# A macaron block with a selective scan: even feed-forward tiles beside the scan steps, and finer, pinned side work

## The chip, the cores and the metric

The kernel runs on one core of one Trainium2 chip. The metric is device time in microseconds (us), the median of three runs. TensorE (PE in the profile, its weight loads PEld) multiplies; VectorE (DVE), ScalarE (ACT) and GpSimd (POOL) do the rest; SyncE (SP) issues all of the loop's DMAs from one queue, in order. The engines run side by side, and each takes its own instructions in order.

## The reference

For x of 4 sequences of 1024 rows and 512 columns, all in float32:

```python
x = x + 0.5 * ffn(layernorm(x))
x = x + mamba(layernorm(x))
x = x + 0.5 * ffn(layernorm(x))          # the same weights as the first

# ffn, inner width 1408
hdn = silu((xf @ gate_w.T) * gate_s) * ((xf @ up_w.T) * up_s)
out = (hdn @ down_w.T) * down_s

# mamba, inner width 1024, state 16
h, gate = split(x @ W_in.T)
h = silu(causal_conv_4_taps(h) + conv_b)
ts, Bm, Cm = split(h @ Wx.T)              # widths 128, 16, 16, each RMS-normed
delta = softplus(ts @ Wdt.T + dt_bias)
s = exp(delta * A) * s + delta * Bm * h   # over the time steps, s is 1024 x 16
y = (s . Cm + D * h) * silu(gate)
out = y @ Wout.T
```

## The kernel before, in words

**Steps.** The 4096 rows are 16 scan steps (`k`, NCS) of 256 rows (T), four to a sequence; a row tile has 128 rows, two to a step. A step has 8 channel tiles of 128 channels (`i`, NI), and each of these 4 units (`g`, NS), so 32 units a step. A unit (`unit`, L517) covers 128 channels and four of the 16 states: states and channels are laid over the partitions, with `rep` holding delta and delta*h of a channel tile four times and `bc` holding B and C. Per unit ACT makes `da` = exp(A*delta) in PSUM (L533, 4 instructions of 256 columns), POOL makes `sb` = delta*h*B (L536, 2 of 512), DVE scans (L540, 4), ACT keeps the last column as `state` (L545), DVE multiplies by C into `pr` (L546, 2), and one unit later PE sums the states with the `fold` matrix into `yps` (`add_up`, L556). After the fourth unit DVE adds D*h into `u` (L562). `gated` (L566, POOL) multiplies `u` by the gate `g`. There are four `da` and four `sb` buffers (two units), three `pr`.

**Work beside the scan.** Everything else is a list of `Work` parts, each with a cost for PE and for DVE. `background(k)` writes the list of step k, and the loop at L738 takes parts from it after each unit as long as the PE cost done lies behind the DVE cost done, or as the next step's parameters must be ready (by unit 22 of 32). The list of step k holds:
- the gate projection of this step (`gate`, L505, ACT copies L509 and one Silu L511), and the output projection of the step before (`tail`, L585, rows written to DRAM as `x2`);
- for step k+1: layer norm, transposes, input projection with the convolution (`prep_conv`, L354, L358, L365), and the small projection with its norms (`prep_params`, L389 to L434), whose last part `turn` stores B and C to DRAM and loads them back, spread over the partitions, as `bc`;
- a feed-forward pass `FFN`: gate products (L243, ACT L257, Silu L262), up products (L243, DVE L274), down products (L291), then `tmp` (L301, DVE) and the sum on POOL (L305). A pass takes up to 512 rows, and its weights (22 + 11 blocks of 256 KB) are loaded anew for each pass.

**Which rows the passes take.** A pass is made of halves of 256 rows, of the first feed-forward (stage 1, which must come before a row's scan) or the second (stage 2, after it). The front has one half; step 0 has two of stage 1; step 1 has one; steps 2 to 13 have one of each stage; step 14 has two of stage 2; step 15 has one; after the last step one is left. In numbers of 128-row tiles: 2, then 4, 2, 4 (x13), 2, then 2. Steps 14 and 15 (`late`) use an order of their own, with the output projection first.

**Softplus.** `head(k, i)`, issued after unit 1 of each odd channel tile for the two tiles three ahead, emits two `dp` products (L461), ACT's Abs, Relu, Exp and Ln (L466 to L469). `rest`, issued one unit later, emits five POOL operations in a row (L472 to L476). `rows` stores the result to DRAM one channel tile later, after unit 1, and `spread` loads it as `rep` at the end of that tile.

**Order.** A scheduler sets the final order of each engine's instructions from priorities, except for those given to `pin`, which keep the order in which they were written. `defer(n, f)` calls f after n more parts that have a PE cost; `settle` calls all that wait. Layer norm (`stats`): DVE statistics (L186, L187), three tiny POOL operations (L188 to L190), and a deferred, pinned ACT instruction (L192); `flip` then transposes on PE (L204), and ACT copies out of PSUM (L207).

Of the kernel before, what the change touches and what calls it, by code (L numbers as in the profile page):

```python
# [13 lines left out]
P = 128  # L14
# [12 lines left out]
Q = 32  # L27
# [5 lines left out]
LEAD = 13  # L33
RING = 15
# [3 lines left out]
def macaron_kernel(ctx: ExitStack, tc: tile.TileContext, a: dict, out: bass.AP):  # L38
# [140 lines left out]
    def stats(src, name):  # L179
# [8 lines left out]
        nc.gpsimd.tensor_scalar(ve, mv[:, 1:2], EPS, None, ALU.add)  # L188
        nc.gpsimd.tensor_tensor(rs, ve, neg_half[:, 0:1], ALU.pow)
        nc.gpsimd.tensor_scalar(nb, mv[:, 0:1], rs, -1.0, ALU.mult, ALU.mult)  # L190
        xn = p3.tile([P, H], F32, tag="xn", name=f"xn{name}")
        cell = [xn, lambda: pin(nc.scalar.activation(xn, src, AF.Identity, bias=nb, scale=rs))]  # L192
        defer(1, lambda: cell[1] and (cell[1](), cell.__setitem__(1, None)))
        return cell

    def flip(cell, dst, name, more=lambda: None):

        xn, norm = cell
        if norm:
            norm()  # L200
            cell[1] = None
# [10 lines left out]
    class FFN:  # L212


        def __init__(self, name, halves):
            self.name, self.halves = name, halves
            self.n = len(halves) * T
            self.x = {}

        def load(self, h):  # L220
            if self.halves[h][0] == 2:
                settle()
                write()
            stage, c = self.halves[h]
            for j in range(J):
                r = c * J + j
                t = self.x[h, j] = p8.tile([P, H], F32, tag="xf", name=f"xf{self.name}_{h}_{j}")
                load(out=t, in_=a["x"][r * P : (r + 1) * P, :] if stage == 1 else x2[r])

        def stats(self, h, j):  # L230
            return stats(self.x[h, j], f"f{self.name}_{h}_{j}")

        def flip(self, xn, h, j):
            if not hasattr(self, "xT"):
                self.xT = p1.tile([P, KH, 2 * T], F32, tag="fxT", name=f"fxT{self.name}")
            o = h * T + j * P
            flip(xn, self.xT[:, :, o : o + P], f"f{self.name}_{h}_{j}")
# [42 lines left out]
        def down(self):  # L280
            parts = [(h, j) for h in range(len(self.halves)) for j in range(J)]
            wd = []

            def part(h, j):
                def emit(w=None):
                    wd.extend(w or [])
                    nm = f"{self.name}_{h}_{j}"
                    op = ps_m.tile([P, H], F32, tag="mm", name=f"fo{nm}")
                    o = h * T + j * P
                    for it in range(NF):  # L290
                        nc.tensor.matmul(  # L291
                            op, lhsT=self.hd[:, it, o : o + P], rhs=wd[it],
                            start=(it == 0), stop=(it == NF - 1),
                        )
                    x = self.x[h, j]
                    tmp = p2.tile([P, H], F32, tag="tmp", name=f"tmp{nm}")
                    stage, c = self.halves[h]
                    r = c * J + j
# [11 lines left out]
                return Work(NF * H, H, emit, [("down_w", it) for it in range(NF)] if h + j == 0 else ())  # L310

            r = [part(h, j) for h, j in parts]
# [65 lines left out]
    def prep_params(k):  # L378
# [46 lines left out]
        def turn():  # L425
# [11 lines left out]
            load(out=row.rearrange("g s t -> (g s) t"), in_=bcT)  # L437
            bc = d["bc"] = p2.tile([P, BC // S, T], F32, tag="bc", name=f"bc{k}")
            for s in range(S):
                load(  # L440
                    out=bc[s * Q : (s + 1) * Q],
                    in_=row[:, s, :].unsqueeze(0).to_broadcast([Q, BC // S, T]),
                )
            d["ready"] = True
# [3 lines left out]
    def head(k, i):  # L448

# [10 lines left out]
        for q in range(2):  # L460
            nc.tensor.matmul(  # L461
                dp[:, q, :], lhsT=w_dt[:, (i + q) * P : (i + q + 1) * P], rhs=d["tsT"],
                start=True, stop=True,
            )
        for q in range(2):
            nc.scalar.activation(z[:, q, :], dp[:, q, :], AF.Abs, bias=dt_b[:, i + q : i + q + 1])  # L466
            nc.scalar.activation(dd[:, q, 0, :], dp[:, q, :], AF.Relu, bias=dt_b[:, i + q : i + q + 1])  # L467
# [14 lines left out]
    def rest(k, i):  # L482

        st[k]["rest", i]()
# [160 lines left out]
    def late(k):  # L645

        return k >= NCS - 2
# [208 lines left out]
```

## Time and profile before

| | us |
|---|---|
| median of 3 runs (3403.05 to 3404.28) | 3403.47 |
| the profiled execution, its own time | 3408.67 |
| its span, first to last instruction | 3406.6 |
| PE / DVE / ACT / POOL busy | 3156.1 / 2434.9 / 2001.4 / 2034.4 |
| DMA traffic | 504.59 MB, mean 148 GB/s |

The profile is of one execution. Busy time is the union of an engine's instructions. In a group's row, the number after the bar is busy time, then the mean ns of one instruction, then the idle time of the engine just before it and what ended it. A line of the waits reads: who waited, for whom, us in total, times, the longest. In the row of a stretch of time, each engine's busy time stands with its number of instructions, then the mean granted TensorE clock as a share of full speed, then the DMA share. In a row in order of time, the bracket at the end is the idle time before it and who ended that. One matrix product in float32 shows as two equal pieces in the profile.

### The profile page before, as it was taken

The numbers are of one execution on the slowest core, as the hardware profiler recorded it, in microseconds if no ns is written. First come the engines' busy times: TensorE is split into PE (matmuls) and PEld (weight loads), VectorE is DVE, ScalarE is ACT, GpSimd is POOL, SyncE is SP. The second block draws the span as 40 slices with busy tenths as digits, with TensorE's granted clock in tenths as the row PEclk, the third lists the DMA queues.
The fourth block names the chain that finished last, engine by engine and source line by source line (L and its number), as shares of the span: only waits on it lengthen the run. The fifth ranks groups of instructions, "written<-read, shape, count | busy, mean of one in ns | idle before, by whom it ended". The sixth has DMA issues, their size and how long they took to land. (4 is left out here: it accounts for less than half of the span.)

```text
span 3406.6 us, 41741 instructions
## 1 busy us (share of the span) xinstructions
PE 3156.1 (93%) x12448; PEld 1609.4 (47%) x12448; DVE 2434.9 (71%) x4202; ACT 2001.4 (59%) x4395; POOL 2034.4 (60%) x1959
## 2 busy tenths in 40 slices
PE   8897676999999999999999999999999999989898
PEld 5534352544444454444445454444545444344445
DVE  1177686687868778786877778687786779757781
ACT  2446654756656575766657475765747576465551
POOL 1266655566665756666575666757566576655760
PEclk9997787999999999999999999999999999999899
DMA  6345454546555554656565465556546555643643
GB/s 201 97 125 138 136 137 123 147 129 185 146 163 156 155 156 117 189 138 171 142 171 161 118 180 137 161 142 171 163 124 177 130 161 142 186 114 100 192 136 105
DMA packets 286417, 504.59 MB, mean 148 GB/s; under 512 B 31984, under 2 KB 50160, under 8 KB 286192
## 3 DMA queue, kind: packets, MB, share of 16 engines
q1 hardware_dynamic: 284608, 501.47, 53.3%
q8 instruction: 100, 1.64, 0.2%
q14 instruction: 125, 1.02, 0.1%
q10 hardware_dynamic: 1584, 0.45, 0.1%
HBM read 442.56 MB, written 59.24 MB: 147 GB/s over the span
## 5 line engine op out<-in xcount | busy, mean ns | idle before, releaser
L536 POOL TENSOR_TENSOR sb<-rep,bc 128x512 f32<-128x512 f32 x1024 | 1280.4, 1273 | 466.0 <-DVE da L540 441.5
L540 DVE TENSOR_TENSOR_SCAN da<-da,state,sb 128x256 f32<-128x256 f32 x1536 | 1060.1, 739 | 263.5 <-ACT da L533 203.4
L533 ACT ACTIVATE da<-rep,a_w 128x256 f32<-128x256 f32 x2048 | 901.3, 470 | 266.2 <-DVE pr L546 249.4
L546 DVE TENSOR_TENSOR pr<-da,bc 128x512 f32<-128x512 f32 x1024 | 667.4, 677 | 77.8 <-ACT state L545 61.8
L243 PE MATMUL up_w<-fxT,w_up_w 128*128 128x512 f32 (+1 forms) x1408 | 607.0, 578 | 18.7 <-issue 13.7
L243 PE MATMUL gate_w<-fxT,w_gate_w 128*128 128x512 f32 (+1 forms) x1408 | 608.5, 577 | 9.6 <-ACT hd L257 4.8
L291 PE MATMUL fo<-w_down_w,hd 128*128 128x512 f32 x1320 | 587.4, 597 | 0.0
L556 PE MATMUL yps<-pr,fold 128*32 128x256 f32 x4096 | 386.6, 401 | 140.0 <-DVE pr L546 117.7
L545 ACT COPY state<-da 128x2 f32<-128x2 f32 x768 | 118.9, 161 | 498.6 <-DVE da L540 490.5
L243 PEld LDWEIGHTS up_w<-fxT,w_up_w 128*128 128x128 f32 x1408 | 260.5, 192 | 304.4 <-issue 288.3
L243 PEld LDWEIGHTS gate_w<-fxT,w_gate_w 128*128 128x128 f32 x1408 | 265.5, 193 | 283.8 <-issue 250.7
L540 DVE TENSOR_TENSOR_SCAN da<-da,sb 128x256 f32<-128x256 f32 x512 | 321.1, 679 | 96.5 <-ACT da L533 69.8
L291 PEld LDWEIGHTS fo<-w_down_w,hd 128*128 128x128 f32 x1320 | 244.6, 191 | 291.3 <-issue 282.7
L556 PEld LDWEIGHTS yps<-pr,fold 128*32 128x32 f32 x4096 | 105.0, 109 | 481.8 <-DVE pr L546 225.7
L472 POOL TENSOR_SCALAR e<-z 128x512 f32<-128x512 f32 x64 | 124.4, 1944 | 214.0 <-ACT z L468 204.9
L505 PE MATMUL gp<-mxT,w_W_in 128*128 128x256 f32 x1024 | 248.7, 392 | 1.9 <-ACT dd L467 1.1
L354 PE MATMUL hp<-mxT,w_W_in 128*128 128x259 f32 x1024 | 244.2, 388 | 5.7 <-issue 2.0
L585 PE MATMUL op<-w_Wout,u 128*128 128x512 f32 x512 | 234.6, 606 | 8.1 <-POOL sb L536 5.3
L365 DVE SCALAR_TENSOR_TENSOR u<-hp,conv_w,u 128x256 f32<-128x256 f32 x384 | 175.1, 473 | 71.2 <-ACT u L358 67.7
L354 PEld LDWEIGHTS hp<-mxT,w_W_in 128*128 128x128 f32 x1024 | 190.0, 190 | 62.3 <-issue 25.3
L505 PEld LDWEIGHTS gp<-mxT,w_W_in 128*128 128x128 f32 x1024 | 190.7, 192 | 57.2 <-issue 21.8
L566 POOL TENSOR_TENSOR u<-u,g 128x256 f32<-128x256 f32 x128 | 92.8, 730 | 196.4 <-DVE u L562 196.2
(114 smaller groups left out, 2744.5 us busy)
## 6 DMA issues: line engine op xcount, KB each, us to landing
rep<-row SPq DMA_DIRECT2D x512, 256.0 KB, 5.6
w_W_in<-in_W_in_dram SPq DMA_DIRECT2D x256, 256.0 KB, 3.1
w_gate_w<-in_gate_w_dram SPq DMA_DIRECT2D x198, 256.0 KB, 3.4
w_up_w<-in_up_w_dram SPq DMA_DIRECT2D x198, 256.0 KB, 3.0
w_down_w<-in_down_w_dram SPq DMA_DIRECT2D x198, 256.0 KB, 2.9
row<-dd SPq DMA_DIRECT2D x128, 256.0 KB, 4.5
w_Wout<-in_Wout_dram SPq DMA_DIRECT2D x128, 256.0 KB, 4.3
bc<-bcd SPq DMA_DIRECT2D x64, 256.0 KB, 4.7
```

Source lines behind the costliest of these rows:

```text
L243: nc.tensor.matmul(o[:, : self.n], lhsT=w[:, k, :], rhs=self.xT[:, k, : self.n], start=(k == 0), stop=(k == KH - 1),)
L291: nc.tensor.matmul(op, lhsT=self.hd[:, it, o : o + P], rhs=wd[it], start=(it == 0), stop=(it == NF - 1),)
L354: nc.tensor.matmul(hp[:, : K - 1 + T], lhsT=w[:, kk, :], rhs=st[k]["xnT"][:, kk, :], start=(kk == 0), stop=(kk == KH - 1),)
L365: pin(nc.vector.scalar_tensor_tensor(u[:, i, :], hp[:, q : q + T], conv_w[:, i, q : q + 1], u[:, i, :], ALU.mult, ALU.add,))
L472: pin(nc.gpsimd.tensor_scalar(e, z, 1.0, 1.0, ALU.add, ALU.subtract))
L505: nc.tensor.matmul(gp[:, :T], lhsT=w[:, kk, :], rhs=st[k]["xnT"][:, kk, K - 1 :], start=(kk == 0), stop=(kk == KH - 1),)
L533: nc.scalar.activation(da[:, j, :], rep[:, h + j, 0, :], AF.Exp, scale=a_w[:, b0 + h + j, g : g + 1])
L536: nc.gpsimd.tensor_tensor(sb, rep[:, hs, 1, :], d["bc"][:, g : g + 1, :].to_broadcast([P, 2, T]), ALU.mult)
L540: nc.vector.tensor_tensor_scan(da[:, j, :], da[:, j, :], sb[:, j, :], 0.0 if first else state[:, b0 + h + j, g : g + 1], ALU.mult, ALU.add,)
L546: nc.vector.tensor_tensor(pr[:, hs, :], da, d["bc"][:, NS + g : NS + g + 1, :].to_broadcast([P, 2, T]), ALU.mult)
L556: nc.tensor.matmul(yp[j * Q : (j + 1) * Q, :], lhsT=fold, rhs=pr[:, j, :], start=(g == 0), stop=(g == NS - 1),)
L585: nc.tensor.matmul(op, lhsT=st[k]["u"][:, i, j * P : (j + 1) * P], rhs=wo[i], start=(i == 0), stop=(i == NI - 1),)
```

## The change

Five things change.

1. The feed-forward passes are made of single 128-row tiles in order of rows. Steps 1, 3, 5, 8, 10 and 12 (`THREE`) get three tiles, all others four, and the pass after the last step four: in tiles 2 (front), then 4, 3, 4, 3, 4, 3, 4, 4, 3, 4, 3, 4, 3, 4, 4, 4, then 4. Steps 14 and 15 lose their own order. The last two rows of the output projection stay in SBUF for the last pass instead of going through DRAM. The gate projection of step 0 moves from the front to the list of step 0.
2. `head` returns a list of eight parts (two of them empty), called `chores`. The first is called after unit 1, the others one by one in the middle of each half unit, before `pr`. Its ACT instructions are pinned. `rows` follows one unit later than before (after unit 2).
3. `stats` emits its POOL operations one part later and its ACT instruction two parts later, all pinned.
4. `gated` is pinned, and the last four channel tiles are always gated in the first units of the next step.
5. The store and the four loads of B and C are deferred by two and three parts.

```diff
-        nc.gpsimd.tensor_scalar(ve, mv[:, 1:2], EPS, None, ALU.add)
-        nc.gpsimd.tensor_tensor(rs, ve, neg_half[:, 0:1], ALU.pow)
-        nc.gpsimd.tensor_scalar(nb, mv[:, 0:1], rs, -1.0, ALU.mult, ALU.mult)
         xn = p3.tile([P, H], F32, tag="xn", name=f"xn{name}")
-        cell = [xn, lambda: pin(nc.scalar.activation(xn, src, AF.Identity, bias=nb, scale=rs))]
-        defer(1, lambda: cell[1] and (cell[1](), cell.__setitem__(1, None)))
+        def roots():
+            pin(nc.gpsimd.tensor_scalar(ve, mv[:, 1:2], EPS, None, ALU.add))
+            pin(nc.gpsimd.tensor_tensor(rs, ve, neg_half[:, 0:1], ALU.pow))
+            pin(nc.gpsimd.tensor_scalar(nb, mv[:, 0:1], rs, -1.0, ALU.mult, ALU.mult))
+        left = [roots, lambda: pin(nc.scalar.activation(xn, src, AF.Identity, bias=nb, scale=rs))]
+        def more():
+            if left:
+                left.pop(0)()
+                defer(1, more)
+        defer(1, more)
...
-            load(out=row.rearrange("g s t -> (g s) t"), in_=bcT)
+            def out_of():
+                load(out=row.rearrange("g s t -> (g s) t"), in_=bcT)
+            def back_in():
+                for s in range(S):
+                    load(out=bc[s * Q : (s + 1) * Q], in_=...)
+            defer(2, out_of)
+            defer(3, back_in)
...
     def head(k, i):
+        return [
+            products,
+            split,
+            logs,
+            lambda: None,
+            lambda: None,
+            lambda: pin(nc.gpsimd.tensor_scalar(e, z, 1.0, 1.0, ALU.add, ALU.subtract)),
+            correct,
+            complete,
+        ]
...
     def unit(k, i, g):
+            if chores:
+                chores.pop(0)()
             nc.vector.tensor_tensor(pr[:, hs, :], da, ...)
...
     def gated(k, i):
-        nc.gpsimd.tensor_tensor(u, u, g_all[:, i, :], ALU.mult)
+        pin(nc.gpsimd.tensor_tensor(u, u, g_all[:, i, :], ALU.mult))
...
-    beside = {0: [(1, 1), (1, 2)]}
-    for k in range(1, NCS):
-        beside[k] = ([(1, k + 2)] if k + 2 < NCS else []) + ([(2, k - 2)] if k >= 2 else [])
-    beside[NCS - 2].append((2, NCS - 3))
-    beside[NCS - 1] = [(2, NCS - 2)]
+    first = [(1, r) for r in range(J, NCS * J)]
+    second = [(2, r) for r in range((NCS - 1) * J)]
+    for k in range(NCS):
+        m = 3 if k in THREE else 4
+        ones = min(len(first), 4 if k == 0 else 3 if k == 1 else 2)
+        twos = m - ones
+        beside[k] = [first.pop(0) for _ in range(ones)] + [second.pop(0) for _ in range(twos)]
+    last = second + [(2, r) for r in range((NCS - 1) * J, NCS * J)]
...
-    front += [turn_m[0], gate_0[2]] + turn_m[1:] + weave(prep_conv(0), gate(0))[0]
+    front += [turn_m[0], gate_0[2]] + turn_m[1:] + prep_conv(0)
...
-                if i == 0 and k and not late(k):
+                if i == 0 and k:
                     gated(k - 1, NI - NS + g)
...
-                if i % 2 == 0 and g == 1 and k2 < NCS:
+                if i % 2 == 0 and g == 2 and k2 < NCS:
                     rows(k2, i2)
                     rows(k2, i2 + 1)
...
-                if i % 2 == 1 and g == 2 and k2 < NCS:
-                    rest(k2, i2)
                 if i % 2 == 1 and g == 1 and k2 < NCS:
-                    head(k2, i2)
+                    chores += head(k2, i2)
+                    chores.pop(0)()
```

The parts of `head` hold the same instructions as before: `products` the two `dp` products, `split` Abs and Relu, `logs` Exp and Ln, `correct` and `complete` two POOL operations each.

## The prediction

> **What bounds the kernel now.** I read the page first, then the busy times by stage, then the waits of one stage, then its instructions in order of time. The page:
>
> ```profile
> span 3406.6 us, 41741 instructions
> PE 3156.1 (93%) x12448; PEld 1609.4 (47%) x12448; DVE 2434.9 (71%) x4202; ACT 2001.4 (59%) x4395; POOL 2034.4 (60%) x1959
> PE   8897676999999999999999999999999999989898
> PEclk9997787999999999999999999999999999999899
> ```
>
> TensorE is busy 93% on average, but slices 4 to 7 (about 255 to 595 us) have 6 or 7 tenths and a clock of 7 or 8 tenths. So there are two kinds of steps. I cut the span at the last `u` (L562) of each step; rows are for step 1, steps 3 and 4, 14, 15, and what follows step 15:
>
> ```profile
> core 0: us, PE busy (x) PEld busy (x) DVE busy (x) ACT busy (x) POOL busy (x), PEclk, DMA share, GB/s
> 376.00:573.20 197.20, 137.36 (x604) 74.12 (x604) 149.86 (x259) 108.11 (x265) 118.61 (x116) 0.81 0.53 153
> 780.90:976.10 195.20, 190.49 (x755) 93.85 (x754) 152.74 (x263) 119.34 (x228) 127.42 (x123) 1.00 0.57 154
> 976.10:1172.80 196.70, 190.47 (x757) 94.09 (x756) 146.37 (x262) 125.37 (x288) 126.50 (x123) 1.00 0.57 155
> 2947.70:3164.10 216.40, 198.26 (x746) 95.88 (x745) 149.36 (x255) 124.95 (x282) 122.79 (x115) 0.96 0.49 136
> 3164.10:3327.40 163.30, 140.93 (x612) 75.76 (x611) 131.27 (x215) 90.53 (x175) 103.09 (x89) 0.91 0.56 158
> 3327.40:3406.60 79.20, 64.46 (x236) 45.52 (x236) 10.87 (x21) 12.04 (x19) 7.81 (x11) 0.92 0.33 103
> ```
>
> Steps 3 to 13 (195 to 199 us each) are TensorE's: idle under 6 us, full clock. Step 1 has half of their feed-forward columns, 53 us less of PE, and takes as long: 60 us of PE idle and a clock of 0.81. Steps 14 and 15 lie between. Where step 1 loses its time:
>
> ```profile
> PE yps L556 <- DVE pr L546: 54.2, 20, 6.5
> POOL u L566 <- DVE u L562: 25.3, 7, 6.1
> ACT z L466 <- PE dp L461: 24.2, 2, 16.5
> DVE da L540 <- ACT da L533: 14.0, 4, 10.9
> DVE da L540 <- POOL sb L536: 13.0, 9, 2.9
> ```
>
> PE waits for the scan (DVE), the scan for `sb` from POOL and `da` from ACT, and these stand behind something else. In order of time, in step 1:
>
> ```profile
> 516.07 1.66 PE L556 MATMUL yps<-pr,fold 128*32 128x256 f32 x8 [6.32 <-DVE pr L546]
> 518.34 0.73 POOL L566 TENSOR_TENSOR u<-u,g 128x256 f32<-128x256 f32 x1 [4.98 <-DVE u L562]
> 520.32 0.76 DVE L540 TENSOR_TENSOR_SCAN da<-da,state,sb 128x256 f32<-128x256 f32 x1 [2.06 <-POOL sb L536]
> 524.22 1.06 PE L556 MATMUL yps<-pr,fold 128*32 128x256 f32 x2 [6.49 <-DVE pr L546]
> ```
>
> The gating `u` on POOL waits 5 us for a `u` just being made, the `sb` behind it come late, the scan starts late, PE stands 6.5 us. The 6.32 us before it follow a softplus burst on POOL (L472 to L476, 503.7 to 512.1 us). PE's gaps of 3.5 to 6.7 us in this step are of these two kinds, or follow ACT's 16.5 us behind `dp`.
>
> **The size of one feed-forward tile.** The end of the chain:
>
> ```profile
> 3363.63 18.99 PE up_we L243 x88
> ```
>
> 88 pieces of 256 columns in 18.99 us: 0.216 us each; the 44 pieces `foe` of 512 columns take 19.0 us (0.432). Time goes by columns, so dividing the same 64 tiles differently removes no PE time; the passes stay 18, so weights are as many. One tile of 128 rows costs 176 gate/up pieces x 0.108 = 19.0, 22 down pieces x 0.432 = 9.5, transposes 0.4: 28.9 us of PE, 2.8 us of DVE (an eleventh share of `hd`, 0.69 `tmp`, 0.83 statistics), some 2 us each of ACT and POOL.
>
> **The change part by part** (us, against the profiled span of 3406.6).
>
> Even tiles. Steps 3, 5, 8, 10, 12 go from four tiles to three; step 1 from two to three; step 15 from two to four; the end from two to four; others keep four. A three-tile step needs 190.5 - 28.9 = 161.6 of PE and about 152 - 3 = 149 of DVE. I counted both kernels' instruction orders between the eight `yps` sums of a step and priced them with the rows: three-tile step, PE 18, 17, 32, 22, 18, 27, 13, 15; DVE (raised 7% to meet its measured busy time) 13, 14, 28, 20, 18, 29, 7, 16. The larger of each pair sums to 165. The same count gives 192 for a four-tile step that measures 196 to 197 (+5), but 150 for step 1, which measures 197 (+47), and 141 for step 15, which measures 163 (+22). So the question is the overhead on 165. I take +11, 176, nearer the four-tile rows, because PE still leads in most tiles and both kinds of stalls are edited (next). Five steps take 984.9 now: 880, -105. Step 1, same load: 177, -20.
>
> Here a rule speaks against the change. Trace: step 1, with its PE gaps of 3.5 to 6.7 us, ran at a clock of 0.81, which is 75 of its 197 us at half rate, and the steps without such gaps at 1.00; at 0.81 a three-tile step would need 161.6/0.81 = 199.5, and nothing would be won. The Trainium skill, "TensorE: Matmul & The Clock Gate", section "Why this matters for your kernels", says gaps above about 3 us drop the clock to half. Taking matmuls out of a step uncovers such gaps. By rule and row of step 1 the five steps bring nothing; at the 0.96 of step 14 they need 168. I stay near the second, since the long gaps have named causes that go.
>
> Softplus in eight parts. No instruction more: per head 2 `dp` pairs, 4 + 2 ACT, 5 POOL (1.94 + 4 x 1.27 = 7.0). `e` now stands 2.5 units after `dp` and, in three of four heads of the new order, an `sb` stands between its POOL parts; at tile 0 nine POOL operations (11 us) still stand together. POOL's wait for `z` (204.9 us in all) goes mostly; ACT's wait for `dp` gets half a unit of distance. Pinned ACT work may make PE's FFN wait for the PSUM bank of `dp`: 0 to 2 a step, in the +11. `row` stores are issued one unit later (5.5 us); they land in 4.5, `rep` in 5.6, and the `rep` is wanted four units (22 us) after its issue: 0, and if that cover were gone POOL and ACT would start the tile late. Seven more table loads, 7 x 1.28 = 9 us on ACT, which is 60% busy: 0.
>
> Gating pinned. In the old order 110 of 128 gatings wait for a fresh DVE result, in the new one 10. POOL's 196.2 us behind `u` go; in PE-bound steps that buys nothing. What is late next is `xf` behind `tmp` (187.8 us on POOL), which the change leaves.
>
> Norms in three. Same instructions, POOL's three and the norm one part later each. POOL's 54.5 us behind `mvf` shrink; a flip may find its norm late: PE waits 12.8 us for that in all now, bound -5 to +5, take 0.
>
> B and C later. Five DMAs move two or three parts (about 4 us each) back on SP. SP's 224.9 us behind `bcT` go; PE waits for no weight transfer anywhere, so 0. They are wanted at the next step, some six units (33 us) on.
>
> Front and step 0. Eight `gp` products (64 pieces x 0.216 = 13.8 of PE) and the gate's Silu go from the front into step 0: -12 there, as PE leads that stretch; step 0 has 41 us of PE idle and fewer stalls, 196 to 188: -8. Step 2 began cold after step 1 (207.7): -11. Step 14 loses its special order and becomes a four-tile step (216.4 to 196): -20. Step 15: count 163 for PE, plus 9: 172, +9.
>
> End. Now 15.4 us from the last `u` to `gate_we`, 57 of matmuls, 5 after. The `x2` store and reload goes (5.3 us of it waiting for the load): about 10, plus 176 x 0.429 + 88 x 0.432 = 113.5, plus 5: 128.5, +49 (say +50).
>
> Sum: -105 -20 -12 -8 -11 -20 +9 +50 = -117, span 3289.6. The profiled run took 3408.67, 2.1 more than its span and 5.2 more than the median 3403.47; on the median's footing 3286.5.
>
> **The rivals.**
> Half the stalls stay: three-tile steps at 187, the overhead of step 15 on 165. Tile 0's burst and `xf` speak for it. Five steps -50, step 1 -10: in all -52, 3351.
> The stalls go entirely: 168, as tight as four tiles. The free end of step 15, where a unit takes 3.8 us of pure DVE, speaks for it. The five -145, step 1 -29, step 0 -14, rest -12 -11 -20 +5 +49: -177, 3226.
> The other side: a step with fewer matmuls isn't shorter, as step 1 shows. The in-order queues lock PE to the scan, PE's gaps pass 3.4 us, half clock holds 196 to 197. Then the six steps bring 0, step 15 takes 196 (+33), the end +50, against -51 elsewhere: +32, 3435. It decides from about 195.5 us per three-tile step, where the six no longer pay the net +8 of the rest.
> That the scheduler undoes the edit is excluded by the order counted above, but for tile 0.
>
> **How the numbers follow.** Likeliest case 0.50 (3286, own range 3260 to 3320), half the stalls 0.22, none 0.15, the other side 0.11, near cancellation 0.02. 0.2% is 6.8 us, about what a measurement of this kernel can tell from no change. Faster 0.86, same 0.03, slower 0.11. The range 3225 to 3372 leaves out the slower side and part of the two middle rivals' far halves.
>
> **What would show it.** Right: three-tile steps of 170 to 182 us with clock above 0.95 and PE idle about 12; POOL's waits of `u` and `e` near zero; step 14 near 196; an end near 128. Wrong: three-tile steps with a clock near 0.8 or PE waiting 40 us for `pr`; four-tile steps over 200; long waits of `da` for `rep` or `bc`.

## The result, and the profile after

The changed kernel takes 3435.47 us (median of 4 runs, 3433.95 to 3437.15) beside 3403.55 for the kernel before: 1.0094 times as long, 95% interval 1.0076 to 1.0111. The forecast was 3286.0, between 3225 and 3372, and faster. The page:

```profile
span 3432.2 us, 41676 instructions
PE 3190.5 (93%) x12448; PEld 1612.8 (47%) x12448; DVE 2434.3 (71%) x4202; ACT 2008.9 (59%) x4402; POOL 2028.4 (59%) x1959
PE   8897699999989998999999899999999899999999
PEclk9998799999999999999999999999999999999999
```

In TensorE's row slices 4 and 5 (about 257 to 429 us) still have 7 and 6 tenths, but the rest of step 1 is filled; yet the span grew by 25.6 us. By steps, cut again at the last `u` (now L588): steps 1, 3, 4, 5, 6, 14, 15, and the end.

```profile
core 0: us, PE busy (x) PEld busy (x) DVE busy (x) ACT busy (x) POOL busy (x), PEclk, DMA share, GB/s
368.90:562.70 193.80, 163.03 (x666) 81.86 (x666) 150.43 (x260) 116.93 (x278) 129.21 (x124) 0.91 0.58 161
770.00:958.00 188.00, 172.14 (x734) 92.09 (x732) 145.62 (x253) 120.77 (x228) 123.67 (x119) 0.95 0.60 164
958.00:1163.80 205.80, 193.96 (x754) 95.32 (x755) 151.05 (x268) 122.84 (x290) 127.25 (x122) 0.98 0.52 142
1163.80:1348.30 184.50, 173.52 (x734) 91.45 (x732) 145.54 (x253) 124.31 (x283) 120.66 (x116) 0.98 0.61 169
1348.30:1558.20 209.90, 198.07 (x757) 96.64 (x758) 159.19 (x271) 126.48 (x294) 132.57 (x129) 0.97 0.51 139
2923.40:3123.90 200.50, 193.10 (x757) 94.84 (x756) 153.91 (x263) 127.28 (x287) 126.88 (x122) 0.99 0.54 151
3123.90:3291.30 167.40, 166.40 (x625) 73.12 (x624) 131.94 (x212) 92.45 (x171) 100.64 (x83) 1.00 0.52 145
3291.30:3432.20 140.90, 132.60 (x312) 58.81 (x312) 15.23 (x23) 19.30 (x23) 12.41 (x19) 0.98 0.21 66
```

Steps 3 and 5 have three tiles and are shorter (188.0 and 184.5); steps 4 and 6 have the tiles they had before and went from 196.7 and 196.9 to 205.8 and 209.9. All steps, in us:

| part | before | predicted change | after | change |
|---|---|---|---|---|
| front and step 0 | 376.0 | -20 | 368.9 | -7 |
| step 1 | 197.2 | -20 | 193.8 | -3 |
| step 2 | 207.7 | -11 | 207.3 | 0 |
| three-tile steps 3, 5, 8, 10, 12 | 984.9 | -105 | 917.7 | -67 |
| four-tile steps 4, 6, 7, 9, 11, 13 | 1182.0 | 0 | 1235.7 | +54 |
| step 14 | 216.4 | -20 | 200.5 | -16 |
| step 15 | 163.3 | +9 | 167.4 | +4 |
| end | 79.2 | +50 | 140.9 | +62 |
| sum | 3406.6 | -117 | 3432.2 | +26 |

Two rows hold most of the error: the four-tile steps (54) and the three-tile steps (38); then step 1 (17), the front (13), the end (12) and step 2 (11). What TensorE waits for in step 4, before and after:

```profile
PE yps L556 <- DVE u L562: 1.5, 1, 1.5
```

```profile
PE yps L582 <- DVE u L588: 3.4, 1, 3.4
PE gate_w L252 <- ACT fxT L217: 3.6, 1, 3.6
```

And VectorE in order of time just ahead of such a `u` in step 6: of the kernel before the scans alone, of the kernel after all up to the `u`:

```profile
1551.40 2.03 DVE L540 TENSOR_TENSOR_SCAN da<-da,state,sb 128x256 f32<-128x256 f32 x3
```

```profile
1540.08 3.32 DVE L564 TENSOR_TENSOR_SCAN da<-da,state,sb 128x256 f32<-128x256 f32 x5
1543.30 0.68 DVE L307 TENSOR_TENSOR tmp<-fo,ds 128x512 f32<-128x512 f32 x1
1543.89 0.47 DVE L588 SCALAR_TENSOR_TENSOR u<-u,d_w,yps 128x256 f32<-128x256 f32 x1
```

The next channel tile's `yps` goes into the one PSUM tile that `u` reads, so TensorE stands until five scans (three before), a `tmp` and the `u` are through. (The tile has two halves, used in turn by the channel tiles, so by the profile the wait is for the tile and not for the same data; two separate tiles were not tried.) GpSimd's waits over the whole run, one of before and three of after, and its longest on a transfer in step 1:

```profile
POOL sb L536 <- DVE da L540: 441.5, 261, 15.7
```

```profile
POOL sb L560 <- DVE da L564: 574.1, 320, 14.4
POOL e L505 <- ACT z L486: 172.1, 37, 10.7
POOL u L592 <- DVE u L588: 16.1, 2, 11.1
```

```profile
379.02 1.26 POOL L560 TENSOR_TENSOR sb<-rep,bc 128x512 f32<-128x512 f32 x1 [20.04 <-DMA bc<-bcd]
```

The gating's wait fell from 196.2 us to 16.1, as predicted; the softplus's only from 204.9 to 172.1; and `sb`'s wait for the scan rose from 441.5 to 574.1: what GpSimd no longer waits for elsewhere it waits for the scan. The last row is new: B and C of step 1, written later, are 20 us late. GpSimd's waits for `rep` grew too, from 6.4 us to 31.5 (five times, the longest 7.7), where the prediction saw full cover; but step lengths don't follow them (with softplus parts and pin alone, see below, step 7 has such a wait of 6.0 us and takes 198.1 us, step 8 has none and takes 198.0).

### The profile page after: what moved, and what is told of

It is laid out like the page before. It is cut to its first block, busy times and chain, and to the rows that moved or that the text cites. A ratio compares the mean times of both kernels' runs of the same rounds, so it can differ in the third digit from the quotient of the medians.

```text
span 3432.2 us, 41676 instructions
## 1 busy us (share of the span) xinstructions
PE 3190.5 (93%) x12448; PEld 1612.8 (47%) x12448; DVE 2434.3 (71%) x4202; ACT 2008.9 (59%) x4402; POOL 2028.4 (59%) x1959
## 5 line engine op out<-in xcount | busy, mean ns | idle before, releaser
L560 POOL TENSOR_TENSOR sb<-rep,bc 128x512 f32<-128x512 f32 x1024 | 1286.4, 1272 | 699.5 <-DVE da L564 574.1
L252 PE MATMUL up_w<-fxT,w_up_w 128*128 128x512 f32 (+1 forms) x1408 | 585.8, 561 | 14.3 <-issue 9.4
L298 PE MATMUL fo<-w_down_w,hd 128*128 128x512 f32 x1276 | 579.7, 608 | 0.0
L582 PE MATMUL yps<-pr,fold 128*32 128x256 f32 x4096 | 396.1, 399 | 150.1 <-DVE pr L572 105.3
L582 PEld LDWEIGHTS yps<-pr,fold 128*32 128x32 f32 x4096 | 105.3, 109 | 486.1 <-DVE pr L572 207.0
L505 POOL TENSOR_SCALAR e<-z 128x512 f32<-128x512 f32 x64 | 124.3, 1942 | 190.0 <-ACT z L486 172.1
L360 PEld LDWEIGHTS hp<-mxT,w_W_in 128*128 128x128 f32 x1024 | 191.4, 191 | 57.9 <-issue 20.4
L311 POOL TENSOR_TENSOR xf<-xf,tmp 128x512 f32<-128x512 f32 x58 | 73.3, 1269 | 163.7 <-DVE tmp L307 163.7
```

Source lines behind the costliest of these rows:

```text
L252: nc.tensor.matmul(o[:, : self.n], lhsT=w[:, k, :], rhs=self.xT[:, k, : self.n], start=(k == 0), stop=(k == KH - 1),)
L298: nc.tensor.matmul(op, lhsT=self.hd[:, it, t * P : (t + 1) * P], rhs=wd[it], start=(it == 0), stop=(it == NF - 1),)
L360: nc.tensor.matmul(hp[:, : K - 1 + T], lhsT=w[:, kk, :], rhs=st[k]["xnT"][:, kk, :], start=(kk == 0), stop=(kk == KH - 1),)
L505: lambda: pin(nc.gpsimd.tensor_scalar(e, z, 1.0, 1.0, ALU.add, ALU.subtract)),
L560: nc.gpsimd.tensor_tensor(sb, rep[:, hs, 1, :], d["bc"][:, g : g + 1, :].to_broadcast([P, 2, T]), ALU.mult)
L582: nc.tensor.matmul(yp[j * Q : (j + 1) * Q, :], lhsT=fold, rhs=pr[:, j, :], start=(g == 0), stop=(g == NS - 1),)
```

## The experiments

Step lengths in all of them are cut at the last `u`. "Full steps" are steps 3 to 13 with four tiles each. Ratios are to the kernel before on the same chip, with the 95% interval.

### Which half of the change costs: the tiles alone, the small edits alone

Theory A: the tiles lose, because a three-tile step gives its saving back at the boundary. Theory B: the tiles pay and the finely issued side work costs. The kernel with the even tiles alone (the changed kernel with the other edits undone):

```diff
-            if chores:
-                chores.pop(0)()
...
-        pin(nc.gpsimd.tensor_tensor(u, u, g_all[:, i, :], ALU.mult))
+        nc.gpsimd.tensor_tensor(u, u, g_all[:, i, :], ALU.mult)
...
-            defer(2, out_of)
-            defer(3, back_in)
+            out_of()
+            back_in()
```

> The kernel before with the even tiles alone (and what belongs to them: no special order in steps 14 and 15, the step-0 gate products moved, the last rows kept in SBUF); softplus, norms, gating and B/C as before. Theory A (the tiles lose: what a three-tile step saves, the four-tile step after it gives back at the step boundary, and the end grows): 3435 to 3460 us, four-tile steps after three-tile ones still near 205 to 210. Theory B (the finer, pinned side work lengthens the TensorE-bound steps by 3 to 10 us each and the tiles alone would pay): 3370 to 3400, four-tile steps back at 196.

Measured 3533.11 us, ratio 1.038 (1.0364 to 1.0395). Steps 5, 6 and 8 (three, four and three tiles):

```profile
1181.00:1380.40 199.40, 172.90 (x731) 91.48 (x729) 147.01 (x253) 125.71 (x287) 126.33 (x122) 0.95 0.57 156
1380.40:1586.30 205.90, 195.80 (x759) 95.92 (x760) 158.79 (x271) 125.47 (x293) 126.41 (x123) 0.98 0.52 142
1780.90:1990.20 209.30, 179.18 (x733) 94.92 (x731) 140.68 (x253) 126.34 (x288) 124.30 (x120) 0.92 0.54 148
```

A step with one tile's TensorE work less (28.9 us by the prediction's count) is as long as before or longer: the five three-tile steps took 1014.9 us (984.9 before), the six four-tile steps 1228.1 (1182.0). The other half, the kernel before with its own tiles and norms, the softplus in eight parts, the gating pinned, B and C later:

> The kernel before with its own tiles and its special order in steps 14 and 15, plus softplus in eight parts, gating pinned, and B and C later; the norms as before. Theory A: at or under the kernel before, 3380 to 3405, with step 1 shorter than its 197 us. Theory B: 3430 to 3460, steps 3 to 13 at 199 to 205 in place of 195 to 199.

Measured 3421.2 us, ratio 1.0055 (1.004 to 1.007): step 1 ended 17 us earlier (555.9 for 573.2), step 15 was 8.5 us shorter, but the full steps took 2202.5 us in all instead of 2166.9. So both halves lose; the tiles lose far more than theory A put on them, and their three-tile steps save nothing that could be given back. In the changed kernel the edits (the norms in three among them, which no run takes alone) give back 98 of the tiles' 130 us. That they help three-tile steps is seen when the softplus alone is set back in the changed kernel:

> The changed kernel with softplus issued as before (ACT's part at once after unit 1, five POOL operations in a row after unit 2, the row stores after unit 1). Theory A: the finer softplus helps where TensorE leaves room, so 10 to 40 us slower than the changed kernel, 3445 to 3475. Theory B, if it is the softplus parts that lengthen the four-tile steps: 3385 to 3415.

Measured 3498.82, ratio 1.0283 (1.0268 to 1.0299): 63 us longer than the changed kernel, 50 of them in the five three-tile steps (967.3 for 917.7).

### Is it the boundary? Three-tile steps in a row

```diff
-THREE = (1, 3, 5, 8, 10, 12)
+THREE = (1, 3, 4, 5, 6, 7)
```

> The changed kernel with the three-tile steps next to each other: THREE = (1, 3, 4, 5, 6, 7) in place of (1, 3, 5, 8, 10, 12). Two boundaries from a three-tile to a four-tile step remain of six. Theory A: each boundary costs about 9 us, so 4 x 9 = 36 less, about 3400. Theory B, or a cost that belongs to the three-tile step itself: no change, 3430 to 3440.

Measured 3459.76, ratio 1.0165 (1.0148 to 1.0182). Steps 3, 4, 5 (three tiles) and 8 (four, the first after them):

```profile
771.30:953.40 182.10, 171.44 (x747) 92.50 (x746) 144.59 (x249) 119.91 (x229) 122.19 (x115) 1.00 0.61 166
953.40:1151.70 198.30, 181.15 (x729) 93.55 (x729) 143.81 (x258) 118.28 (x280) 123.34 (x119) 0.96 0.57 156
1151.70:1348.60 196.90, 178.83 (x733) 93.81 (x734) 150.62 (x259) 122.64 (x288) 124.18 (x119) 0.96 0.56 151
1739.70:1946.70 207.00, 195.66 (x757) 96.18 (x758) 151.57 (x270) 124.05 (x292) 129.30 (x126) 0.97 0.53 144
```

Neither theory's total came: this order is 24 us slower than the changed kernel. Only the first three-tile step is short; the next four take 198.3, 196.9, 194.2 and 196.9, as long as full ones, and the first full step after them takes 207.0. Of the first one's 13 us the first full step pays back 6 to 8: part of it is a loan, work put off past the last `u`. VectorE's instructions show it: 249 in the first one, 258 and 259 in the next two, 270 in the full step behind them, where a full step before has 262 or 263. In the changed kernel, where the two kinds alternate, each three-tile step after a full one looks short and each full step after it long, so they are read in pairs: (3, 4), (5, 6), (8, 9), (10, 11) and (12, 13) take 391.1 us on average, 394.3 before, and two full steps under the same edits (steps 9 to 14 of grouped) 401.4. The tile less saves 10 us a pair there and 4 us a step in succession, where 21 were predicted.

### Does a step get shorter with still less TensorE work?

The grouped order, with two tiles computed in steps 3 to 7 and the third one's rows left out:

```diff
         beside[k] = [first.pop(0) ...] + [second.pop(0) ...]
+        if k in (3, 4, 5, 6, 7):
+            beside[k] = beside[k][:2]
```

> The grouped order again (three tiles in steps 1, 3 to 7), but steps 3 to 7 compute only the first two tiles of their pass: the second feed-forward rows of the third tile are left out there, so some 24 us of TensorE work is gone from each of five steps. Grouped took 196 us for such a step in steady succession. Theory S (a step has a floor of about 190 us set by the scan engines whatever TensorE does, as the step before with two tiles, 197 us, suggests): steps 4 to 7 stay at 188 to 197 us, the total falls by under 30 us from grouped (3460), to 3430 or more. Theory C (TensorE's products and the scan hold each other up, so that less TensorE work shortens the step even where TensorE idles): steps 4 to 7 fall to 172 to 182 us and the total by 70 to 110 us, to 3350 to 3390.

Measured 3424.01 us, ratio 1.0062 (1.0042 to 1.0083). Steps 4 and 5:

```profile
936.30:1127.00 190.70, 155.92 (x705) 92.69 (x706) 141.06 (x256) 119.44 (x287) 121.64 (x114) 0.87 0.55 154
1127.00:1318.10 191.10, 157.85 (x705) 93.78 (x705) 147.56 (x255) 119.14 (x287) 121.69 (x114) 0.88 0.55 155
```

Theory S holds: steps 4 to 7 stay at 190.7 to 191.4 us. Another tile of TensorE work gone (28.9 us by the prediction's count) takes 3 to 8 us off each. The total fell by 36 us rather than by under 30, since step 3, again the first of the row, lost 12 of its own (169.8 us; the full step behind the row took 211.8).

### Which engine's work is the floor? Half of one at a time

The grouped order, in steps 3 to 7 with half of `pr` left out (VectorE), half of `sb` (GpSimd), or one exp instead of two (ScalarE). The first as a diff; the others likewise:

```diff
-            nc.vector.tensor_tensor(pr[:, hs, :], da, ...)
+            if h == 0 or k not in (3, 4, 5, 6, 7):
+                nc.vector.tensor_tensor(pr[:, hs, :], da, ...)
...
-                yp[...], lhsT=fold, rhs=pr[:, j, :],
+                yp[...], lhsT=fold, rhs=pr[:, j % 2 if k in (3, 4, 5, 6, 7) else j, :],
```

> The grouped order with half of the pr products left out in steps 3 to 7 (the sum reads the first half twice, so TensorE does the same): 32 fewer VectorE operations a step, 0.65 us each, 21 us off VectorE's 151. Grouped took 198.3, 196.8, 194.3, 196.9 in steps 4 to 7. If VectorE's own work in the scan sets the length: 174 to 184 us each. If it is the waits of the queues on TensorE's products: 190 us or more.

> The grouped order with half of the sb products left out in steps 3 to 7 (the second pair of scans reads the first pair's): 32 fewer GpSimd operations a step, 1.27 us each, 41 us off GpSimd's 125. GpSimd waits 40 us a step for the scan already. If GpSimd sets the length: 180 us or less in steps 4 to 7. If not: 192 to 198 as in grouped.

> The grouped order with one exp over both halves of a pair, under the first half's factor, in steps 3 to 7: 64 fewer ScalarE instructions a step, of 0.47 us for 256 elements; for 512 an estimate is 0.68 (a ln or exp of the softplus has that size), so 16 us off ScalarE's 120. If ScalarE's rate of exps sets the length: 180 to 186 us in steps 4 to 7. If not: 192 to 198.

Measured 3447.63, 3462.94 and 3479.11 us, two runs each (grouped 3459.76). Step 5 in the three:

```profile
1136.10:1334.20 198.10, 173.22 (x735) 94.36 (x735) 131.08 (x226) 122.18 (x289) 125.92 (x121) 0.93 0.55 152
```

```profile
1150.20:1347.70 197.50, 179.94 (x733) 94.36 (x734) 150.71 (x259) 122.68 (x288) 84.52 (x87) 0.96 0.54 151
```

```profile
1152.80:1359.90 207.10, 187.14 (x733) 95.33 (x734) 152.26 (x259) 111.19 (x225) 125.63 (x120) 0.93 0.52 144
```

VectorE works 20 us less, GpSimd 40, ScalarE 11, and steps 5 to 7 of none are shorter than in grouped by more than 1 us. Two things stay unexplained: step 4 of the first took 183.6 us for 198.3, and the single exp lengthened steps 5 to 7, to 203 to 207. With VectorE lighter, its wait for the exps in step 5 took back 13 of the 20 us; grouped first, then half of `pr`:

```profile
DVE da L564 <- ACT da L557: 22.9, 5, 8.2
```

```profile
DVE da L564 <- ACT da L557: 36.3, 6, 13.3
```

So no one engine's amount of work sets steps 5 to 7. Followed back from the last `u` of step 7 to that of step 3 (each instruction to what released it, or to the one ahead of it on its engine), grouped's chain spends 115 us a step on TensorE, 32 on VectorE, 24 on ScalarE, 8.5 on GpSimd; the two-tile kernel's 104, 32, 25 and 15: it passes from engine to engine. What the exps stand behind, seen in the two-tile kernel, ScalarE in order of time:

```profile
1343.42 0.37 ACT L533 COPY g<-gp 128x256 f32<-128x256 f32 x1 [1.36 <-PE gp L529]
1345.86 0.47 ACT L266 ACTIVATE hd<-gate_w,gate_s 128x256 f32<-128x256 f32 x1 [2.07 <-PE gate_w L252]
1347.64 0.37 ACT L533 COPY g<-gp 128x256 f32<-128x256 f32 x1 [1.31 <-PE gp L529]
1349.37 0.37 ACT L533 COPY g<-gp 128x256 f32<-128x256 f32 x1 [1.35 <-PE gp L529]
1349.76 1.28 ACT L557 ACT_TABLE_LOAD   x1
1351.05 2.86 ACT L557 ACTIVATE da<-rep,a_w 128x256 f32<-128x256 f32 x7
```

ScalarE goes from one TensorE product to the next, 6 us of it idle, and then loads a table (1.28 us), with the exps queued behind; VectorE then stands 7.98 us for them. Elsewhere in this step (step 6) TensorE stands for the scan instead, 23.0 us in all. I tried to take out the wait by moving the copies:

```diff
-                nc.scalar.copy(g_all[:, i, :], gp[:, :T])
+                def out():
+                    pin(nc.scalar.copy(g_all[:, i, :], gp[:, :T]))
+                    ...
+                defer(2, out)
```

> The grouped order, with ScalarE's copy of each scan-gate product (g) written two parts of TensorE work later and pinned there, so that the exps don't stand behind a copy whose product isn't done. In grouped three-tile steps in succession took 198.3, 196.8, 194.3, 196.9. If the exps standing behind copies that wait for TensorE set their length: 185 to 191 us each, the waits of g on TensorE near zero, total 3425 to 3445. If the scan's own work is the floor (or the wait moves to the next copy, hd): 193 to 198 us each and the total within 12 us of 3460.

Measured 3530.13, ratio 1.0368 (1.0352 to 1.0383): worse than either theory, with steps 4 to 7 at 206.5 to 215.1 us. `g` hardly waited (2.1 us for 8.3), but `hd` did (49.6 us for TensorE in 420 us from late in step 5 on, 26.0 in steps 6 and 7 of grouped, 393 us), and VectorE's `u` waited 34.6 us for `yps` there (14.5). The pattern of waits is seen, but how much of a step's length it makes, and so why a step keeps its 191 to 198 us, stays open.

### What costs in the full steps: softplus, gating, or B and C

First a direct try on the late `u`: the sum's products written half a unit earlier in the changed kernel.

```diff
+            if h == 0 and summed:
+                add_up()
...
-                if len(summed) > 1:
-                    add_up()
```

> The changed kernel with the products of a scan unit's sum (yps) written half a unit earlier, so that u, the read of the sum by VectorE, is queued behind one or two scans rather than up to five. Theory U (in four-tile steps TensorE loses its time in gaps of 2 to 3.5 us at yps behind a late u, each followed by half clock): the gaps on u shrink under 2 us, the four-tile steps fall from 205 to 210 us towards 197 to 200 and the total from 3435 to 3380 to 3410. Theory R (TensorE's loss comes from running dry at the end of the steps and from the scan's own lateness): yps then waits for pr instead, the same or more, and the total stays within 15 us of 3435 or rises.

Measured 3438.42, ratio 1.0105 (1.009 to 1.012). It decides nothing on `u`: at the place shown above VectorE's order was the same, five scans, `tmp`, `u`, and the gap stayed 3.4 us. Then the edits one by one on the kernel before: the softplus in eight parts alone; with the gating pinned as well; and with all three edits, but the softplus parts and the pin only in steps 0, 1 and 15.

> The kernel before with the softplus in eight parts alone: gating, norms, B and C as before. If the pinned softplus parts push u behind more scans: steps 3 to 13 at 199 to 201 us and the total at 3415 to 3425, as with all fine edits. If it is the pinned gating that does it: steps 3 to 13 stay at 195 to 198 us and the total falls to 3375 to 3400, with the front and step 0 shorter by about 15 us.

> The kernel before with the softplus in eight parts and the gating pinned; B and C and the norms as before. The softplus alone gave 3398 with steps 3 to 13 at 195 to 199 us; with the pinned gating and the later B and C also there (the fine edits alone) it was 3421 with steps 3 to 13 at 199 to 201.5. If the pinned gating lengthens the full steps: 199 to 201 us each and 3420 to 3430 in all. If the later B and C do: steps 3 to 13 stay at 195 to 199 us and the total is 3390 to 3402.

> The kernel before, its tiles unchanged, with the softplus in eight parts and the gating pinned only in steps 0, 1 and 15 and the front, where TensorE isn't the bound; in steps 2 to 14 both stand as before; B and C are written later everywhere. With the fine edits everywhere the front and step 0 lost 17 us, step 15 lost 8 us, and steps 2 to 14 gained about 40. Theory U (the fine edits cost only where TensorE is full): 3375 to 3385. Theory B2 (the later B and C or the shifted state of step 2 on cost it, not the softplus and the pin): steps 3 to 13 stay at 199 to 201 us and the total at 3410 to 3425.

| kernel | us | ratio (interval) | last `u` of step 1 | steps 3 to 13 | step 15 |
|---|---|---|---|---|---|
| before | 3403.55 | 1 | 573.2 | 2166.9 | 163.3 |
| softplus in parts | 3398.15 | 0.9986 (0.998 to 0.9993) | 567.4 | 2162.7 | 160.3 |
| and gating pinned | 3401.68 | 0.9994 (0.9987 to 1.0) | 543.9 | 2186.9 | 160.4 |
| and B and C later | 3421.20 | 1.0055 (1.004 to 1.007) | 555.9 | 2202.5 | 154.8 |
| the last, softplus and pin in steps 0, 1, 15 only | 3415.32 | 1.0035 (1.0022 to 1.0047) | 557.4 | 2192.2 | 154.9 |

The softplus costs nothing in the full steps. The pin brings 23 us by step 1 and costs 24 in the full steps; B and C later, added to it, cost 12 by step 1 and 16 in the full steps and bring 6 in step 15. These costs don't simply add: in the last row, without pin and softplus parts in steps 2 to 14, the later B and C go with full steps that are 25 us longer than before, and not 16. Step 6's waits for `u`, with the softplus alone, with the pin, and (as a row in order of time) with all three:

```profile
PE yps L569 <- DVE u L575: 1.5, 1, 1.5
```

```profile
PE yps L569 <- DVE u L575: 2.2, 1, 2.2
```

```profile
1557.77 1.08 PE L576 MATMUL yps<-pr,fold 128*32 128x256 f32 x8 [3.44 <-DVE u L582]
```

```profile
1554.00:1561.20 7.20, 3.76 (x12) 1.38 (x12) 7.20 (x13) 1.79 (x6) 4.82 (x6) 0.68 0.13 36
1561.20:1568.00 6.80, 6.80 (x14) 2.86 (x13) 5.92 (x10) 3.42 (x9) 5.84 (x6) 0.84 0.73 196
```

The last two rows are TensorE around that gap: it costs 3.4 us, and the half clock that makes the 0.68 and 0.84 begins in the gap and outlasts it by 5.6 us, while TensorE is busy. The same two edits, undone in the changed kernel:

> The changed kernel with the gating's position left to the scheduler, as before. If the pinned gating is what lengthens the full steps: four-tile steps shorter by 3 to 5 us each, the total 3400 to 3418. If it has no part in it: 3430 to 3440. If, as the prediction had it, the pin takes a stall off POOL and so off the exps and the scan: three-tile steps longer by 5 us or more without it, the total 3450 or more.

> The changed kernel with B and C written at once, as before. If the later B and C are what lengthens four-tile steps beside the boundary: steps 7 and 14 fall from 198 and 200 to 195 to 197 us, the four-tile steps after three-tile ones from 205 to 210 to 200 to 206, the gaps at yps on a late u shrink under 2 us, and the total is 3400 to 3415. If they have no part in it: 3428 to 3440.

Without the pin 3470.32, ratio 1.0198 (1.0183 to 1.0213): the pin is worth 35 us there, 22 in the three-tile steps and 13 in the four-tile ones. So its cost in full steps doesn't carry over to full steps behind lighter ones; only steps 7 and 14, which follow full ones, are shorter without it by more than half a us (0.7 and 2). With B and C at once 3429.22, ratio 1.0076 (1.0061 to 1.0091), 6 us less: step 1, without its 20 us wait, 181.3 for 193.8, the four-tile steps 12 us less, but the front and step 0 8 us longer and the three-tile steps 10.

### A version that beats both

With the softplus parts everywhere: B and C later for the first two chunks alone; or the gating pinned in steps 0 and 1 alone; or this and B and C later for the last chunk alone.

```diff
+PINNED = (0, 1,)
...
-        nc.gpsimd.tensor_tensor(u, u, g_all[:, i, :], ALU.mult)
+        w = nc.gpsimd.tensor_tensor(u, u, g_all[:, i, :], ALU.mult)
+        if now[0] in PINNED:
+            pin(w)
...
+            if k == NCS - 1:
+                defer(2, out_of)
+                defer(3, back_in)
+            else:
+                out_of()
+                back_in()
```

> The kernel before with the softplus in eight parts, and B and C written later for the first two chunks of tokens alone (those that the front and step 0 prepare); gating and norms as before. With all fine edits the last u of step 1 came at 555.9 us, with the softplus alone at 567.4, before at 573.2. If the later B and C give the 11 us of these steps: last u of step 1 at 554 to 558, the other steps as with the softplus alone, 3384 to 3390 in all, the shortest of all kernels here. If the pinned gating gives them: 567 and 3395 to 3400.

> The kernel before with the softplus in eight parts everywhere and the gating pinned in steps 0 and 1 alone. With the softplus alone the last u of step 1 came at 567.4 us and steps 3 to 13 took 2163 us; with the gating pinned everywhere it came at 543.9 and they took 2187. If the pin's gain (steps 0 and 1) and its cost (full steps) are separate: 544 and 2163, 3374 to 3380 in all. If the gain is borrowed from the steps after (the scan only runs ahead, and TensorE has the same work left): 3394 to 3402.

> As the kernel with the gating pinned in steps 0 and 1, and B and C of the last chunk (prepared in step 14) written later. With the later B and C step 15 took 155 us, without 160. If that is theirs: 5 us below that kernel. If step 15 was short because of the state that the fine edits left before it: the same as that kernel within 2 us.

Measured 3391.09, ratio 0.9965 (0.9953 to 0.9977); 3389.89, ratio 0.996 (0.9948 to 0.9973); and 3382.54, ratio 0.9934 (0.9922 to 0.9947). The last is the shortest of all, 21 us under the kernel before, 53 under the changed one. Its steps 1, 6 and 15:

```profile
368.60:552.90 184.30, 138.37 (x620) 75.23 (x620) 149.38 (x259) 110.97 (x274) 118.28 (x118) 0.87 0.56 160
1352.80:1551.20 198.40, 192.67 (x757) 94.62 (x756) 153.34 (x262) 126.87 (x289) 126.76 (x123) 0.99 0.56 153
3147.00:3301.70 154.70, 136.59 (x613) 74.14 (x612) 128.35 (x210) 90.32 (x175) 100.47 (x87) 0.93 0.59 168
```

Step 15 lost the 6 us and steps 3 to 13 stayed at 2167.4, but the last `u` of step 1 came at 550.3 and 552.9 rather than at 544: of the 29 us that softplus and pin had brought there together, 20 to 23 are left, so gain and cost are separate only in the main (step 1 took 184.3 us, 177.6 with the pin in all steps). B and C later for the first two chunks brought 5 us by step 1 where 11 were hoped for.

## Why the prediction was wrong

**The step that failed first: "I take +11, 176", the overhead on 165.** The sum priced a three-tile step as the larger of TensorE's and VectorE's work between two sums, plus a little. The runs show that in steady succession a step which also prepares the next one takes 191 us with two tiles, 194 to 198 with three, and 195 to 199 (199 to 201.5 under the same edits) with four, and that with half of one engine's scan operations left out steps 5 to 7 were no more than 1 us shorter. What keeps it there is seen only as a pattern of waits between the engines; its cause stays open. The overhead belonged at +30, between the +22 and +47 that the same count had given for the two steps where TensorE wasn't full; these were the nearest rows, and I chose the four-tile rows (+5) over them. The 917.7 measured in the changed kernel mixes shorter steps with loans that the next ones paid.

**"Others keep four", at nothing.** The four-tile steps cost 54, and 51 of these lie in the five that follow a three-tile step (1037.6 us for 986.8); step 7, with a full step ahead of it, took 198.1. The profile before already had such a step: step 2, behind the lighter step 1, took 207.7 us.

```profile
573.20:780.90 207.70, 195.28 (x760) 95.84 (x760) 159.10 (x271) 125.94 (x294) 128.87 (x125) 0.97 0.51 142
```

Its VectorE counts are those of step 6 after (271 instructions, 159.19 us). The prediction took its 11 us as a gain (they stayed: 207.3) and put no such term on the five new places, where 10 us each were lost. Both begin alike: at the end of the lighter step TensorE has nothing else ready, stands for the scan, and then takes 9.00 and 8.90 us for the full step's first 16 gate pieces, which at 0.429 would be 6.9. Step 2 before and step 6 after:

```profile
579.86 1.06 PE L556 MATMUL yps<-pr,fold 128*32 128x256 f32 x2 [6.65 <-DVE pr L546]
```

```profile
1352.43 1.06 PE L582 MATMUL yps<-pr,fold 128*32 128x256 f32 x2 [4.17 <-DVE pr L572]
```

Of step 6's 13 us the tiles alone make 9.0 (205.9 for 196.9) and the edits alone 4.6 (201.5).

**Edits costed at nothing because the page shows slack.** The softplus was rightly nothing in full steps. The pin and the later B and C were not: they order GpSimd's and SyncE's work, for which TensorE does not wait, but the scan moves against the sum and `u` comes later, from 1.5 us of TensorE gap to 2.2 with the pin (still behind three scans) and 3.4 with both (behind five). Six units of cover for B and C were wrong in step 1 outright: 20.0 us late. Without that wait step 1 took 181.3 us, near its price of 177, though the front and step 0 gave 8 of the 12 us back. The sign of the pin depends on the step: a gain in light steps and, in the changed kernel, in the full steps behind them; a cost in full steps behind full ones.

**The clock rule.** The prediction set it aside for three-tile steps, and there that was right: the changed kernel's ran at 0.95 (step 3) and 0.98 (step 5). It bore on the steps where it wasn't looked for: in steps 3 to 13 half clock follows 8 of the 11 gaps on `u` over 1.5 us in the changed kernel and all ten with the edits alone, and none of the ten (1.5 us) before. The Trainium skill ("TensorE: Matmul & The Clock Gate", "Why this matters for your kernels") puts the limit near 3 us; here a third of the gaps of 1.5 to 2 us already cost (last section), and the measurement decides.

**The rival that landed, 3435, has the right number and only half of its mechanism.** That a step with fewer matmuls isn't shorter held in steady succession. But it put 0 on the six steps (measured -70 in place), 196 on step 15 (measured 167.4, TensorE idle 1.0), and named half clock for the three-tile steps; it had no term for the four-tile steps (+54), and of the 51 us that it kept from the other edits 23 came. That these errors cancel is luck.

**The end, +50.** It took +62. The chain of waits:

```profile
3310.53 40.86 PE gate_we L252 x88
3351.39 37.77 PE up_we L252 x88
3389.16 37.78 PE foe L298 x88
```

Gate and up products took 78.6 us where 176 x 0.429 = 75.5 were priced (the gate products began at less than full clock, 0.85 in their first 19.5 us, and took 0.464 us a piece; the up and down products came at 0.429, as priced). That is 3 of the 12. The other 9 lie ahead: `gate_we` begins 19.2 us after the last `u`, where the sum had about 10.

**What held.** Step 14's order (-16 for -20), step 15 (167.4 for 172), the gating's waits, the weights never late, the table loads.

## What to carry to other kernels

Before pricing a step by the engine that will lead it, look for a step in the same trace that already has that load: here step 1, with half the feed-forward work and the same 197 us, said that less TensorE work alone would not shorten a step, the count that said otherwise missed that step by 47 us, and step 2 behind it showed what a full step pays. Such a step is a warning and no floor: with softplus parts and pin, and its two tiles, step 1 took 177.6. When neighbouring iterations change in opposite directions, add them in pairs or run a long row of one kind before calling either a gain. An edit that reorders an engine with slack should be measured stage by stage: on the kernel before, the same pin was worth 23 us up to step 1 and cost 24 in eleven full steps.

## What the runs showed of the hardware

Half clock comes after shorter gaps than I had taken, and not always. Over ten profiles here (before, after, grouped, and those with the edits alone, singly or in part: the four of the table of edits and the three of the last experiment) I took TensorE's gaps in steps 3 to 13 that have no other gap over 0.7 us within 12 us before and 8 us after, and looked whether a half-clock record begins between 1.5 us before and 4 us after TensorE resumes:

| gap, us | gaps | followed by half clock |
|---|---|---|
| 0.7 to 1.0 | 45 | 0 |
| 1.0 to 1.5 | 220 | 2 |
| 1.5 to 2.0 | 65 | 22 |
| 2.0 to 2.5 | 23 | 10 |
| 2.5 to 3.0 | 14 | 9 |
| 3.0 to 3.5 | 18 | 15 |
| over 3.5 | 6 | 6 |

Several of the ten kernels share most of their steps, so these cases are not independent. All twenty profiles give the same picture: 4 of 455 below 1.5 us, then 39 of 126, 21 of 41, 28 of 37, 50 of 57, and 28 of 42 over 3.5 us, where in 13 more the clock was already at half. The records of the table last 3.4 us or twice that. So, as an estimate, a gap that grows from 1.5 to 3.4 us, as on `u` here, costs 2 us of waiting and, most times, up to 1.7 or 3.4 us more for work at half speed; step 6 with all three edits grew by 4.6.
